# Ternary weights prepared by compares on GpSimd and means on ScalarE, and a timetable three times as fine, in a state-space and feed-forward kernel

## The chip, the core and the metric

The kernel runs on one core of a Trainium2 chip. The core has five engines, each with an instruction queue of its own that it works through in order: TensorE (PE, matrix products, with the loading of its weights shown apart as PEld), VectorE (DVE), ScalarE (ACT), GpSimd (POOL) and SyncE (SP, which here only issues DMAs). They meet through semaphores alone: an instruction that needs a result waits at the head of its queue, and all that stands behind it waits too. The metric is the device time of one execution in microseconds, the median of the runs.

## The reference

The input is x[2, 4096, 256] in float32. Two layers with residuals are applied:

```
x = x + layernorm(ssm(layernorm(x)))
x = x + layernorm(ffn(layernorm(x)))
```

The state-space layer projects to 2 x 512 channels (a path x and a gate z) and takes B, C (16 states each), dt and lam from silu(x). For each of 512 channels and 16 states it runs, over 4096 tokens, `h = dA*h + u`, and y is the sum over states of `h*C`. Then y is gated with silu(z) and projected back to 256. The feed-forward layer is 256 to 1024 to 256 with gelu and a layernorm between, and its weights are ternary:

```python
def ternary_quant(w):
    scale = 1.0 / jnp.clip(jnp.mean(jnp.abs(w)), 1e-05)
    wq = jnp.clip(jnp.round(w * scale), -1.0, 1.0) / scale
    return w + jax.lax.stop_gradient(wq - w)
```

So each weight becomes -1, 0 or 1 times the mean magnitude of its matrix.

## The kernel before, in words

**Blocks and units.** The 8192 tokens are cut into 16 blocks of 512 (`NB`), 8 to a batch. In a block the scan covers 512 channels x 16 states, that is 64 *units* of 128 rows by 512 tokens (`NU` = 64): 4 channel quarters j, times 4 groups q of states, times 4 units c. A group is four units. For each unit ACT computes the decays `da` = exp(A dt) into PSUM (`decay`, L924, by `special`, L217; `da` has four buffers). For each pair of units POOL multiplies B and v into a group's tile `g` (`inputs`, L929, instruction L934; three buffers). DVE then runs one hardware scan per unit (`unit_scan`, L940): for the first `SPLIT[q]` units of a group (2, 1, 2, 1) it writes into `da` (L947), for the others into `g` (L950). The product with C is DVE's for the former (`product_v`, L964, and a copy of the last column, L965) and POOL's, in place in `g`, for the latter (`product_g`, L960), after ACT has copied their last column to `hl` (`last`, L954). PE adds up the states (`sum_states`, L976, into `y`), which frees the `g` tile, and DVE gates (`gate`, L986). `start_y` (L970) puts the skip term into `y` first.

**The rest of a block** is put between the units: for the block after the next layernorm, projections, softplus, rotation and so on (`plan_ahead`: `a_stats`, `project`, `keep`, `silu_x`, ..., `load_c`), and for the block before the output projection and the feed-forward layer (`plan_behind`: `out_project`, `out_square`, `residual`, `h_stats`, `ffn_1`, `ffn_keep`, `gelu`, `ffn_2`, `ffn_sums`, `ffn_out`, ..., `finish`). dt, v, B and C go through HBM and come back spread over the rows (`load_ch`: dtr and vr; `load_bc`: b and c); SP issues those DMAs in program order.

**What sets the order.** The queues' order is written out by hand. The main loop (L1312) goes from unit to unit. At each it asks for the decays up to 3 units and the inputs of up to 3 units ahead (`AHEAD_DA`, `AHEAD_U`), issues the scan, then what lags (`behind`, L1265, with one lag in units for each kind in `LAG`), and then every piece of the plans whose unit has come (`AT`, `AT_FIRST` for block 0, `W_AT` for the weights; `Plan.run`, L1119).

**The weights.** In block 0 a third plan (`plan_weights`, L1242) prepares the constant weights between the units. `centre_out` (L355) takes from each row of `wo` its mean. `ternary` (L369) loads a matrix into half of a wide tile, takes the mean magnitude (ACT with an accumulator, then a PE product with ones), and on DVE rounds by adding and subtracting a large constant, clips, scales, and forms w + (wq - w). `weights_1` and `weights_2` then fold in the layernorms' gains (`gains`) and offsets (`offsets`, PE), and for the second matrix subtract the mean over the hidden axis (`hidden_mean`, `centre`) and over the outputs (`output_mean`, `finish`, instruction L481). All of that elementwise work is on DVE.

Of the kernel before, what the change touches and what calls it, by code (L numbers as in the profile page):

```python
# [8 lines left out]
F32 = mybir.dt.float32  # L9
# [5 lines left out]
P = 128  # L15
# [23 lines left out]
AHEAD_DA, AHEAD_U = 3, 3  # L39
# [3 lines left out]
LAG = {"product_v": 2, "last": 4, "product_g": 5, "gate": 9, "start": 7, "sum": 8}  # L43

W_AT = (11, 13, 20, 23, 24, 24, 27, 28, 28, 30, 33, 33, 38, 41, 46, 51, 51, 51, 52, 52, 55, 58, 59, 62, 63)
LOAD_FIRST = 8
AT = {
    "a_stats": (2, 2),
    "a_power": (2,),
    "a_offset": (3,),  # L50
    "a_apply": (3, 4),
    "a_turn": (4, 5),
    "a_evict": (5, 5),
    "project": (5, 7, 11, 11, 19, 21, 21, 21),
    "keep": (7, 9, 11, 13, 20, 21, 22, 24),
    "silu_x": (13,),
    "bc_project": (17, 17),
    "bc_take": (19,),
    "dt_project": (25,),
    "bc_square": (22,),  # L60
    "bc_power": (24,),
    "dt_row": (30,),
    "dt_spread": (33,),
    "softplus": (33,),
    "bc_scale": (33,),
    "dt_turn": (35, 35, 35, 37),
    "dt_keep": (35, 35, 36, 37),
    "dt_sum": (43,),
    "angles": (43,),
    "diag_lam": (29,),  # L70
    "diag_rem": (29,),
    "silu_z": (49,),
    "sines": (49,),
    "rotate_a": (52,),
    "rotate_b": (52,),
    "bc_turn": (52,),
    "bc_store": (54,),
    "dot_sum": (53,),
    "dot_shift": (53,),
    "dot_take": (60,),  # L80
    "weigh": (37, 37, 46, 46),
    "weigh_x": (39, 39, 47, 50),
    "over": (49,),
    "over_x": (52,),
    "spread": (60,),
    "carry": (61,),
    "diag_dot": (64,),
    "skip": (64, 66, 67, 67),
    "skip_x": (65, 66, 67, 67),
    "load_dt": (41,),  # L90
    "load_v": (40,),
    "load_b": (59, 59, 58, 61),
    "load_c": (55, 59, 59, 64),
    "x_load": (5,),
    "out_project": (12, 12),
    "out_square": (16, 16),
    "out_power": (16, 16),
    "residual": (18, 18),
    "h_stats": (18, 18),
    "h_power": (18,),  # L100
    "h_offset": (20,),
    "h_apply": (20, 20),
    "h_turn": (21, 25),
    "h_evict": (24, 25),
    "ffn_1": (25, 29, 31, 31, 34, 34, 41, 42),
    "ffn_keep": (27, 29, 31, 32, 34, 34, 42, 42),
    "gelu": (40, 45),
    "ffn_2": (47, 50, 52, 62),
    "ffn_sums": (48, 52, 57, 64),
    "ffn_out": (48, 52, 58, 65),  # L110
    "ffn_square": (60, 58, 63, 66),
    "ffn_power": (60, 66),
    "ffn_scale": (62, 66),
    "finish": (64, 66),
# [9 lines left out]
    "project": (-59, -58, -57, -56, 0, 0, 0, 0),  # L124
    "keep": (-58, -57, -56, -55, 0, 0, 0, 0),
# [16 lines left out]
    "silu_z": (2,),  # L142
# [8 lines left out]
    "weigh": (-41, 0, 2, 0),  # L151
    "weigh_x": (-35, 0, 3, 4),
    "diag_dot": (0,),
    "skip": (0, 4, 4, 4),
    "skip_x": (2, 5, 5, 5),
    "load_dt": (-34,),
    "load_v": (-32,),
    "load_b": (-31, -20, 0, 0),
    "load_c": (-30, -20, 0, 0),
# [4 lines left out]
def mamba_ffn_kernel(  # L164
# [190 lines left out]
    def centre_out():  # L355
        wom = small.tile([P, NJ], F32, tag="rows", name="wom")
        nc.vector.tensor_reduce(wom, wo, AX.X, ALU.add)
        nc.vector.tensor_scalar_mul(wom, wom, 1.0 / DM)
        for j in range(NJ):
            nc.vector.tensor_scalar_sub(wo[:, j, :], wo[:, j, :], wom[:, j : j + 1])  # L360
# [8 lines left out]
    def ternary(src, wide, nk, width):  # L369
# [27 lines left out]
        def round_():  # L397
            nc.vector.tensor_scalar(q, w, t["scale"], ROUND, ALU.mult, ALU.add)
            nc.vector.tensor_scalar(q, q, ROUND, -1.0, ALU.subtract, ALU.max)

        def clip():
            nc.vector.tensor_scalar(q, q, 1.0, t["inv"], ALU.min, ALU.mult)

        def apart():
            nc.vector.tensor_sub(q, q, w)

        def together():
            nc.vector.tensor_add(w, w, q)

        return w.rearrange("p (k n) -> p k n", k=nk), [  # L410
            load, magnitude, total, scales, round_, clip, apart, together,
        ]

    def weights_1(wide):
        w, steps = ternary(w1T, wide, 2, HID)
        t = {}

        def offsets():
            t["pb"] = mm_tile([P, NH], "pb1")
            for f in range(NH):  # L420
                for kk in range(2):
                    nc.tensor.matmul(
                        t["pb"][:, f : f + 1],
                        lhsT=w[:, kk, f * P : (f + 1) * P],
                        rhs=lb1[:, kk : kk + 1],
                        start=(kk == 0),
                        stop=(kk == 1),
                    )

        def gains():  # L430
            nc.vector.tensor_add(b1c, t["pb"], b1c)
            for kk in range(2):
                nc.vector.tensor_scalar_mul(w1q[:, kk, :], w[:, kk, :], g1[:, kk : kk + 1])

        return steps + [offsets, gains]

    def weights_2(wide):
        w, steps = ternary(w2T, wide, NH, DM)
        t = {}

        def offsets():
            t["pb"] = mm_tile([P, DM], "pb2")
            for f in range(NH):
                nc.tensor.matmul(
                    t["pb"],
                    lhsT=lb2[:, f : f + 1].to_broadcast([P, P]),
                    rhs=w[:, f, :],
# [4 lines left out]
        def gains():  # L452
            nc.vector.tensor_add(b2bc, t["pb"], b2bc)
            for f in range(NH):
                nc.vector.tensor_scalar_mul(w[:, f, :], w[:, f, :], g2[:, f : f + 1])
# [10 lines left out]
        def centre():  # L466
            m = p1.tile([P, DM], F32, tag="junk", name="m2")
            nc.vector.tensor_scalar_mul(m, t["pm"], 1.0 / HID)
            nc.vector.tensor_sub(w, w, m[:, None, :].to_broadcast([P, NH, DM]))

        def output_mean():
            wm = small.tile([P, NH + 1], F32, tag="wm", name="wm", bufs=1)
            nc.vector.tensor_reduce(wm[:, 0:NH], w, AX.X, ALU.add)
            nc.vector.tensor_reduce(wm[:, NH : NH + 1], b2bc, AX.X, ALU.add)
            nc.vector.tensor_scalar_mul(wm, wm, 1.0 / DM)
            t["wm"] = wm

        def finish():
            wm = t["wm"]
            for f in range(NH):  # L480
                nc.vector.tensor_scalar_sub(w2q[:, f, 0:DM], w[:, f, :], wm[:, f : f + 1])  # L481
            nc.vector.tensor_scalar_sub(b2bc, b2bc, wm[:, NH : NH + 1])

            nc.vector.memset(w2q[:, :, DM : DM + 1], 1.0)

        return steps + [offsets, gains, hidden_mean, centre, output_mean, finish]
# [625 lines left out]
    class Plan:  # L1112
# [6 lines left out]
        def run(self, unit):  # L1119
            while self.pieces and self.pieces[0][0] <= unit - self.start:  # L1120
                self.pieces.pop(0)[2]()
# [5 lines left out]
    def plan_ahead(s, prev):  # L1127
# [3 lines left out]
        else:  # L1131
            plan = Plan(AT, prev.k * NU)
# [64 lines left out]
    def plan_behind(s):  # L1197

        plan = Plan(AT, (s.k + 1) * NU)
# [65 lines left out]
    def behind(m):  # L1265
# [121 lines left out]
```

## Time and profile before

| | |
|---|---|
| median of 3 runs | 2062.05 us (2061.23 to 2062.91) |
| profiled execution | 2063.1 us, its span 2061.4 us |
| first scan of block 0 | 64.5 us |
| first scan of block 1 | 224.3 us |
| last scan | 1983.0 us |
| busy DVE, POOL, PE, ACT | 1799.0, 1791.1, 1741.9, 1622.9 us |
| DVE's scans, L950 and L947 | 706.1 and 423.0 us |
| POOL's inputs L934 and products L960 | 1017.4 and 631.7 us |
| ACT's decays, L217 da | 690.3 us |

The span is that of the instructions on the chip; the execution's time has 1.7 us around it. A row of the profile is a group of like instructions: line, engine, operation, tiles written and read, shapes, count, then busy time and mean duration in ns, then the idle time of that engine just before them and who ended it. A wait is written "A <- B": A stood until B was done.

### The profile page before, as it was taken

To read this page: it belongs to the slowest core of one execution; us is meant where nothing else is said; L and a number is where in the kernel's file an instruction comes from. 1 tells how busy PE (TensorE), PEld (TensorE's weight loads), DVE (VectorE), ACT (ScalarE), POOL (GpSimd) and SP (SyncE) were. 2 spreads that over 40 slices of the span, in tenths; PEclk is the share of its full clock that TensorE was granted. 3 is DMA by queue.
4 is the path that set the end of the run, shared out by engine and by line. 5 is a ranking of instruction groups with operands and counts; after the bars stand their busy time and mean duration, and the time that the engine had idled before them with its cause. 6 is when DMAs were issued, how large, how long until landed. Compare 5 with 4: busy or idle time off the path is not lost.

```text
span 2061.4 us, 28008 instructions
## 1 busy us (share of the span) xinstructions
PE 1741.9 (85%) x8638; PEld 1040.5 (50%) x8638; DVE 1799.0 (87%) x2806; ACT 1622.9 (79%) x3301; POOL 1791.1 (87%) x1163
## 2 busy tenths in 40 slices
PE   6765788998898898988889899988888898888677
PEld 3423446464554546455454646455454645555255
DVE  1789989899899989999898989989898999989950
ACT  5655587888979798888979788897979888796743
POOL 3578799998999999999999999999999999999950
PEclk7867799999999999999999999999999999998899
DMA  4832536444564545445463644446454544556200
GB/s 80 203 82 74 129 78 153 112 106 111 126 153 100 137 105 135 110 114 134 123 147 86 151 112 114 110 121 150 107 131 109 132 109 110 136 123 142 44 21 10
DMA packets 155687, 233.37 MB, mean 113 GB/s; under 512 B 30129, under 2 KB 55793, under 8 KB 155537
## 3 DMA queue, kind: packets, MB, share of 16 engines
q1 hardware_dynamic: 153408, 230.80, 46.6%
q0 software_dynamic: 544, 0.71, 0.2%
q8 instruction: 68, 1.11, 0.2%
q14 instruction: 83, 0.67, 0.1%
q10 hardware_dynamic: 1584, 0.07, 0.1%
HBM read 188.51 MB, written 42.99 MB: 112 GB/s over the span
## 4 chain that ended last, share of the span: by engine, by line
DVE 37%; ACT 31%; PE 11%; issue 9%; DMA 6%; POOL 5%; SPq 1%; DVEq 0%; POOLq 0%; ACTq 0%
DVE g L950 15%; ACT da L217 10%; DVE da L947 8%; ACT L217 4%; DVE g L964 4%; ACT L213 3%; DMA vr<-v_d 3%; ACT h L217 3%; POOL g L960 2%; PE ph L1022 2%; PE pf L1044 2%; DMA xpre<-in_L_attn_x_dram 2%; POOL g L934 2%; ACT dt L217 2%; ACT zs L217 1%
## 5 line engine op out<-in xcount | busy, mean ns | idle before, releaser
L934 POOL TENSOR_TENSOR g<-b,vr 128x1024 f32<-128x1024 f32 x512 | 1017.4, 2001 | 13.3 <-DMA c<-bc_d 13.3
L217 ACT ACTIVATE da<-dtr,aneg 128x512 f32<-128x512 f32 x1024 | 690.3, 685 | 191.2 <-DVE g L950 183.5
L960 POOL TENSOR_TENSOR g<-c,g 128x1024 f32<-128x1024 f32 (+1 forms) x256 | 631.7, 2468 | 108.6 <-ACT hl L954 105.3
L950 DVE TENSOR_TENSOR_SCAN g<-da,ini,g 128x512 f32<-128x512 f32 x560 | 706.1, 1267 | 3.5 <-ACT da L217 3.5
L947 DVE TENSOR_TENSOR_SCAN da<-da,ini,g 128x512 f32<-128x512 f32 x336 | 423.0, 1279 | 72.4 <-POOL g L934 43.9
L1044 PE MATMUL pf<-w2q,h 128*128 128x257 f32 x1024 | 315.7, 390 | 39.9 <-DVE o L1082 26.0
L976 PE MATMUL y<-g,fold 128*32 128x512 f32 x2048 | 312.0, 639 | 42.9 <-ACT y L970 23.8
L562 PE MATMUL pz<-oT_a,wi 128*128 128x512 f32 x512 | 275.1, 677 | 30.9 <-ACT zs L576 28.7
L1022 PE MATMUL ph<-oT_h,w1q 128*128 128x512 f32 x512 | 259.6, 645 | 37.3 <-ACT dt L217 33.7
L964 DVE TENSOR_TENSOR g<-da,c 128x512 f32<-128x512 f32 x384 | 255.6, 666 | 0.0
L1053 PEld LDWEIGHTS pf<-h 128*128 128x128 f32 x1024 | 195.3, 191 | 27.5
L1053 PE MATMUL pf<-h 128*128 128x128 f32 x1024 | 197.4, 275 | 0.0
L562 PEld LDWEIGHTS pz<-oT_a,wi 128*128 128x128 f32 x512 | 101.9, 214 | 182.6 <-issue 95.2
L1022 PEld LDWEIGHTS ph<-oT_h,w1q 128*128 128x128 f32 x512 | 93.9, 197 | 187.2 <-issue 90.0
L1044 PEld LDWEIGHTS pf<-w2q,h 128*128 128x128 f32 x1024 | 155.7, 192 | 57.2 <-DVE o L1082 36.0
L976 PEld LDWEIGHTS y<-g,fold 128*32 128x32 f32 x2048 | 46.0, 110 | 160.6 <-POOL g L960 41.5
L815 PE MATMUL pw<-ddot,dtT 128*128 128x128 f32 (+1 forms) x512 | 85.7, 317 | 43.2 <-DVE dx L878 27.4
L994 PE MATMUL po<-wo,zs 128*128 128x256 f32 x512 | 116.8, 387 | 0.0
L994 PEld LDWEIGHTS po<-wo,zs 128*128 128x128 f32 x512 | 97.4, 193 | 28.0 <-ACT da L217 5.0
L217 ACT ACT_TABLE_LOAD x80 | 102.6, 1283 | 1.4
L815 PEld LDWEIGHTS pw<-ddot,dtT 128*128 128x128 f32 x512 | 73.2, 212 | 60.4 <-DVE dx L878 28.8
L213 ACT ACT_TABLE_LOAD x80 | 102.6, 1283 | 1.2
(206 smaller groups left out, 2375.0 us busy)
## 6 DMA issues: line engine op xcount, KB each, us to landing
dtr<-dt_d SPq DMA_DIRECT2D x256, 256.0 KB, 5.5
vr<-v_d SPq DMA_DIRECT2D x256, 256.0 KB, 7.3
dt_d<-dt SPq DMA_DIRECT2D x64, 256.0 KB, 3.9
v_d<-v SPq DMA_DIRECT2D x64, 256.0 KB, 2.1
b<-bc_d SPq DMA_DIRECT2D x256, 64.0 KB, 2.1
c<-bc_d SPq DMA_DIRECT2D x256, 64.0 KB, 2.2
xpre<-in_L_attn_x_dram SPq DMA_DIRECT2D x16, 512.0 KB, 4.5
xpost<-in_L_attn_x_dram SPq DMA_DIRECT2D x16, 512.0 KB, 3.9
```

Of the source, the lines that this page charges most:

```text
L217: nc.scalar.activation(dst, src, f, **kw)
L562: nc.tensor.matmul(s.pz[e], lhsT=wi[:, kk, e * P : (e + 1) * P], rhs=s.na.oT[:, kk, :], start=(kk == 0), stop=(kk == 1),)
L934: nc.gpsimd.tensor_mul(s.g[j, q][:, hs, :], s.bcq[0, q][:, None, :].to_broadcast([P, 2, T]), s.ch[j, "vr"][:, hs, :],)
L947: nc.vector.tensor_tensor_scan(da, da, g, ini, ALU.mult, ALU.add)
L950: nc.vector.tensor_tensor_scan(g, da, g, ini, ALU.mult, ALU.add)
L960: nc.gpsimd.tensor_mul(g, s.bcq[1, q][:, None, :].to_broadcast([P, NG - n, T]), g)
L964: nc.vector.tensor_mul(s.g[j, q][:, c, :], da, s.bcq[1, q])
L976: nc.tensor.matmul(s.ys[j][c * G : (c + 1) * G, :], lhsT=fold, rhs=g[:, c, :], start=False, stop=(q == NQ - 1), skip_group_check=True,)
L994: nc.tensor.matmul(s.p2[h][:, i, :], lhsT=s.zs[j][:, c * P : (c + 1) * P], rhs=wo[:, j, :], start=(j == 0), stop=(j == NJ - 1),)
L1022: nc.tensor.matmul(s.ph[f], lhsT=w1q[:, kk, f * P : (f + 1) * P], rhs=s.nh.oT[:, kk, :], start=(kk == 0), stop=(kk == 1),)
L1044: nc.tensor.matmul(po[:, 0 : DM + 1], lhsT=gT, rhs=w2q[:, f, :], start=(f == 0), stop=(f == NH - 1), skip_group_check=True,)
L1053: nc.tensor.matmul(po[:, DM + 1 :], lhsT=gT, rhs=gT, start=False, stop=False, skip_group_check=True,)
```

## The change

**The weights.** With s the scale, round(s w) clipped to -1..1 is the compare s w > 0.5 less the compare s w < -0.5. Both compares (128x2048) and their difference (two halves) are now made by GpSimd; the factor 1/s is not multiplied into the matrix but into the gains and the offsets (`factors`, a few columns). The form w + (wq - w) goes. The gains are applied by ScalarE, which sums each row in the same instruction (`accum_out`), so that the separate reductions over the outputs go too; the mean of a row after centring is that sum less the sum of the hidden mean. ScalarE also takes the means of `wo` and subtracts means (as a bias). VectorE keeps the scale, two additions of biases and one subtraction of the hidden mean, now in one instruction that reads PSUM.

**The timetable.** A unit now has three places: before the decays and inputs ahead are issued, between them and the scan, and after the scan; a block has 192. All tables are written in places. The lags of `last`, `product_g` and `sum` differ from group to group, those of `gate` and `start` from quarter to quarter. Decays and inputs are asked for 2 units ahead instead of 3.

```diff
-AHEAD_DA, AHEAD_U = 3, 3
+AHEAD_DA, AHEAD_U = 2, 2
-LAG = {"product_v": 2, "last": 4, "product_g": 5, "gate": 9, "start": 7, "sum": 8}
-LOAD_FIRST = 8
+LAG = {
+    "product_v": (6,),
+    "last": (24, 19, 23, 11, 15, 14, 19, 20, 16, 12, 17, 15, 12, 14, 15, 11),
+    "product_g": (31, 20, 29, 21, 24, 21, 23, 22, 23, 16, 22, 20, 19, 16, 17, 20),
+    "gate": (33, 32, 31, 33),
+    "start": (28, 24, 25, 26),
+    "sum": (36, 29, 29, 26, 29, 22, 26, 27, 33, 23, 27, 24, 30, 25, 27, 30),
+}
+W_AT = (17, 24, 60, 69, 70, 79, 90, 90, 110, 117, 122, 122, 129, 129, 129, 130, 133, 133, 136, 136, 137, 137, 138, 143, 147, 153, 169, 175, 185)
+LOAD_FIRST = 6
 AT = {
...
-    "silu_x": (13,),
+    "silu_x": (42,),
-    "softplus": (33,),
+    "softplus": (89,),
-    "out_square": (16, 16),
-    "out_power": (16, 16),
-    "residual": (18, 18),
+    "out_square": (46, 48),
+    "out_power": (48, 48),
+    "residual": (50, 51),
-    "ffn_keep": (27, 29, 31, 32, 34, 34, 42, 42),
-    "gelu": (40, 45),
+    "ffn_keep": (84, 92, 111, 114, 117, 118, 126, 127),
+    "gelu": (116, 133),
-    "ffn_sums": (48, 52, 57, 64),
-    "ffn_out": (48, 52, 58, 65),
+    "ffn_sums": (143, 156, 172, 190),
+    "ffn_out": (143, 158, 173, 191),
...
     def centre_out():
...
+            nc.scalar.activation(
+                junk, wo[:, j, :], AF.Copy, scale=-1.0 / DM, accum_out=wom[:, j : j + 1]
+            )
+        for j in range(NJ):
+            nc.scalar.activation(wo[:, j, :], wo[:, j, :], AF.Identity, bias=wom[:, j : j + 1])
...
+        def above():
+            nc.gpsimd.tensor_scalar(q, w, t["scale"], 0.5, ALU.mult, ALU.is_gt)
+
+        def below():
+            nc.gpsimd.tensor_scalar(w, w, t["scale"], -0.5, ALU.mult, ALU.is_lt)
+
+        def signs(half):
+            n = NH * DM // 2
+            hs = slice(half * n, half * n + n)
+            nc.gpsimd.tensor_sub(q[:, hs], q[:, hs], w[:, hs])
+
+        def factors():
+            for name, col in cols.items():
+                t[name] = small.tile([P, nk], F32, tag=f"wc{nk}{name}", name=name, bufs=1)
+                nc.gpsimd.tensor_scalar(t[name], col, t["inv"], None, ALU.mult)
...
+            for f in range(4 * h, 4 * h + 4):
+                nc.scalar.activation(
+                    w[:, f, :],
+                    q[:, f, :],
+                    AF.Copy,
+                    scale=t["g"][:, f : f + 1],
+                    accum_out=t["row"][:, f : f + 1],
+                )
...
+            nc.vector.scalar_tensor_tensor(
+                w,
+                t["pm"][:, None, :].to_broadcast([P, NH, DM]),
+                -1.0 / HID,
+                w,
+                ALU.mult,
+                ALU.add,
+            )
...
+    def at_place(place):
+        behind(place)
+        for plan in plans:
+            plan.run(place)
...
+        at_place(3 * base)
+        if cur is not None:
             ahead(base + AHEAD_DA, "da", 1, decay)
             ahead(base + AHEAD_U, "u", 2, inputs)
+        at_place(3 * base + 1)
+        if cur is not None:
             unit_scan(cur, j, q, c)
-        behind(base)
-        for plan in plans:
-            plan.run(base)
+        at_place(3 * base + 2)
```

`behind` now looks a place up in a table `due`, made once from `LAG`. The other entries of `AT` and `AT_FIRST` are all rewritten in the same way: most move by a few units, softplus and what hangs on it three to six units earlier, the last two `weigh` some sixteen later; the z projections and the skips of block 0 move from its first unit to within its first six.

## The prediction, made before the result

> **What bounds the kernel now.** I read the page first. Four engines are busy for 79 to 87% of the span, so no total decides, and each stage has to be read by itself.
>
> ```profile
> span 2061.4 us, 28008 instructions
> PE 1741.9 (85%) x8638; PEld 1040.5 (50%) x8638; DVE 1799.0 (87%) x2806; ACT 1622.9 (79%) x3301; POOL 1791.1 (87%) x1163
> ```
>
> Next the busy time by stretch, cut at the first scan of block 0 (64.5 us), of block 1 (224.2), of one later block (578.3 to 696.9), and of the last block (columns: stretch, its length, then busy time and count of PE, PEld, DVE, ACT, POOL, then the granted clock).
>
> ```profile
> 64.50:224.20 159.70, 101.27 (x439) 59.96 (x437) 148.12 (x199) 85.64 (x159) 125.86 (x67) 0.71 0.42 106
> 578.30:696.90 118.60, 105.67 (x542) 63.22 (x538) 109.76 (x173) 100.77 (x207) 110.25 (x72) 0.96 0.50 121
> 1875.00:1983.00 108.00, 80.37 (x376) 44.67 (x376) 101.74 (x145) 71.69 (x149) 103.17 (x54) 0.86 0.33 73
> ```
>
> By the starts of every 64th scan, blocks 1 to 14 take 1650.8 us (117.9 each), the last 107.9, and from its last scan to the end there are 78 us. A middle block has 109.8 us of DVE and 110.3 of POOL work: both are all but full, and 8 us of the block are waits. Block 0 has 148 us on DVE and 42 us more length than the others: it carries the weights.
>
> Whose waits they are, over the six blocks 342 to 1050 us (columns: total, times, longest); first DVE's own, then POOL's largest.
>
> ```profile
> DVE da L947 <- POOL g L934: 19.6, 12, 1.7
> DVE da L947 <- ACT da L217: 11.2, 12, 1.5
> DVE o L1082 <- ACT rsf L217: 9.6, 12, 0.8
> DVE zs L986 <- PE y L976: 1.7, 3, 1.0
> ```
> ```profile
> POOL g L960 <- ACT hl L954: 33.1, 32, 1.9
> ```
>
> Per block: 3.3 us for POOL's inputs, 1.9 for ACT's decays, 1.6 for ACT's root, 0.6 others. POOL loses 5.5 us at its products, waiting for ACT's copy of the last column, which stands behind decays that wait for DVE: a ring.
>
> Last, the weights in block 0 (lines of 64.5 to 224.2 us), and what they do to POOL meanwhile:
>
> ```profile
> L481 DVE TENSOR_SCALAR w2q<-wide,wm 128x256 f32<-128x256 f32 x8 | 6.6, 891 | 0.0
> L408 DVE TENSOR_TENSOR wide<-wide 128x2048 f32<-128x2048 f32 x2 | 6.4, 3178 | 0.0
> L360 DVE TENSOR_SCALAR wo<-wo,wom 128x256 f32<-128x256 f32 x4 | 6.3, 1639 | 0.0
> ```
> ```profile
> 130.20 4.04 POOL L960 TENSOR_TENSOR g<-c,g 128x1024 f32<-128x1024 f32 x1
> 134.21 3.22 POOL L802 TENSOR_TENSOR mix<-mix,ident 128x512 f32<-128x512 f32 x1
> 517.94 1.18 POOL L802 TENSOR_TENSOR mix<-mix,ident 128x512 f32<-128x512 f32 x1
> ```
>
> The first two ran while DVE did the 128x2048 operations of w1 (129.4 to 136.3 us); the third is the same instruction in a later block. The 256-wide L360 and L481 took 1.64 and 0.89 us where L455, of that size, took 0.35: the two engines hold each other up.
>
> **Part 1, the weights (block 0).** Removed from DVE by the rows of that stretch: L481 6.6, L408 6.4, L360 6.3, L405 5.2, L398 3.2, L402 2.7, L399 2.5, L473 2.3, L455 2.2, L433 2.0, L358 1.4, L357 1.2 and four small ones (L468, L474, L482, L475) 1.3: 43.3 us. The subtraction of the hidden mean stays (3.5 us, now straight from PSUM), as do the scales and two bias adds. DVE in block 0: 148.1 - 43.3 = 104.8 us.
>
> Added to ACT: 4 sums of 256 (0.40 + 0.19 for the accumulator, row L1091) and 4 corrections (0.50, L1102) of wo; 2 products of 1024 (1.1, from 0.67 for 512 in L1033); 8 products with sums (0.69), 2 means (0.57), 9 corrections (0.50): 18 us. ACT: 85.6 + 18 = 104, beside the rest.
>
> Added to POOL: four compares of 128x2048, four subtractions of 128x1024 (2.00, row L934) and seven small ones (1.4): 9.4 us and the compares. No row has such a compare. Below: POOL's COPY took 0.29 us for 128 and 0.61 for 512 columns, which gives 1.9 for 2048. Above: its TENSOR_SCALAR took 0.22 for 32 and 0.55 for 128, which gives 7.2; but that 0.55 lay beside DVE's three adds of `fold`, one of which took 0.33 instead of 0.19. A two-input row gives 4.0 (twice 2.00). I take 3.0, between the copy and the two-input row, and keep 1.9 and 7.2. Weights on POOL: 9.4 + 12.0 = 21.4. What POOL gets back is its slowing by DVE's weights: 1.0 + 2.0 + 2.0 on g, 2.0 on mix, 0.8 on bc, 5.0 + 1.9 on cs, t and bdotc (2.36 us for one that takes 0.32): 14.8. POOL in block 0: 125.9 - 14.8 + 21.4 = 132.5 us, the longest of the four. It also waits: for the scale of w2, behind its load (landing 5.7 to 13.6 us), ACT's magnitude (1.9) and PE; for ACT's row sums; at its products. Behind the first compare of w2 stand POOL's inputs of units 46 to 49, and DVE's scans wait for those. I take 7 us, a middle block's (33.1 us at L960 and 11 in small ones over six blocks), bounds 3 and 12. Block 0: 139.5 instead of 159.7, **20 us less**; bounds 29 less (1.9 a compare, 3 of waits) and 2 more (7.2 and 12).
>
> A rule speaks against this part. The Trainium skill, "GPSIMD Engine Reference", section Engine selection, sends elementwise work to VectorE and calls GpSimd about twice as slow with two inputs, near line rate with one. The trace agrees on two inputs (2.00 us for 1024 on POOL, 2.3 at best for 2048 on DVE, L405). By the page alone the compares would be about 1.8 us each, an estimate, and block 0 some 5 us shorter than mine; the engine that is full decides here. "SBUF — State Buffer", section "Who interferes with whom", says that VectorE in a two-port mode or with two SBUF inputs locks GpSimd out; the 3.22 us against 1.18 shows it.
>
> **Part 2, the timetable (15 blocks).** Not one operation of a middle block changes, only the order on the queues, so its floor stays at 110.3 us. I laid both kernels' queues for one block side by side and added up the rows' durations.
>
> *DVE waiting for POOL (3.3 us).* If both queues ran without gaps, from the first input and scan on, POOL's inputs before would come up to 2.4 us late (unit 36), while the fourth group's product stands 0.1 us too early for its scan: no shift between the engines serves both, 2.5 us are lost, 3.3 are measured. In the new order the worst are 2.3 (unit 56) and a product with 1.2 us in hand: 1.1. The last column's copy now stands one to ten places before its product instead of one unit. I take 1.6 off; bounds 0 and 3.3.
>
> *DVE waiting for decays (1.9).* 1.4 of it is unit 16: silu of x (table, 1.91, copy, table: 4.7 us of ACT) stood one unit before it. It now stands before da 15, and out_square behind da 16; counting ACT's rows from the scan that frees da 14's buffer, da 15 comes at 6.1 us and its scan can start at 6.3. 1.4 off, with no slack (bounds 0 and 1.9).
>
> *Root (1.6).* Two of four ffn_out stood right behind ffn_sums; now one does: 0.8 off (bounds 0 and 1.6).
>
> *New.* Products move back, from 5 units behind to 16 to 31 places (three to a unit), so a g buffer comes free later. Between a group's product and the inputs that reuse its buffer POOL had at least 5.9 us of other work, and now 2.0 (groups 6 and 7), 2.9 and 3.0 (0 and 2). In it PE must do four y matmuls (the last six of the trace take 1.9 us). I add 0.8; bounds 0 and 4.0 (2.0 at two groups).
>
> Sum: -1.6 - 1.4 - 0.8 + 0.8 = -3.0 a block, 42 for fourteen, 1.5 for the last: **43.5 us less**. SP's queue: its loads of b, c, dtr and vr keep their order within a few units and land before use in both lists; v of quarters 2 and 3 is stored some 15 units later, yet behind the loads that units 16 on need and 14 units ahead of its own; nothing taken. Start: z projections and skips move to either side of the first scan, which waits 11.9 us for inputs anyway, and dtr and vr of the next quarter are asked for two units sooner: nothing, bounds 3 either way. Tail (78 us): gelu 0 goes ahead of ffn_keep 4; PE then stands 2 us for a buffer and gelu 1 ends as before: nothing, bounds 3.
>
> **The sum.** The profiled execution took 2063.1 us, 1.7 outside its span; 2063.1 - 20.2 - 43.5 = 1999.4. The median of the runs is 1.05 below the profiled one: 1998.
>
> **Rivals.**
> *The timetable only moves the waits.* Both engines are 93% full, so a wait removed in one place may return at the next. Against it: the margins above. 2062 - 20 = 2042. Chance 0.14.
> *The compares are dear.* At 7.2 us or more POOL is the bound of block 0 at 161 us. For it: the one row of that operation. 2062 - 43 = 2019. Chance 0.13.
> *PE late with the sums (slower).* With a g buffer held longer, POOL waits wherever PE comes late to the y matmuls. For it: PE waited up to 3.3 us for ACT's softplus (ph, 19.5 us in six blocks), and group 6's sum now stands behind the dt turns that need it. Against: that group's product starts 5.2 us after its last scan, when the softplus should be past. At 2.5 us for four groups POOL loses 10 a block, 5 more than it saves: 2062 + 70 - 20 = 2112. It decides from 5.2 us a block on (the 3.8 saved, and 20/14). Chance 0.10.
> *It does nothing*: the weights' chain eats what DVE gives up and the order is neutral: 2062. Chance 0.03.
>
> **How the numbers follow.** Both gains: 0.60, at 1998. The cheapest ends (6.7 a block, 29 in block 0) give 1936, the dearest of the likely case about 2045. 1945 to 2045 leaves out some 0.05 below and 0.13 above. A measurement here can tell 0.2% (4 us). Faster 0.87, same 0.03, slower 0.10.
>
> **What would show it.** After: first scan of block 0 to that of block 1 near 140 us, with DVE near 105 and POOL near 132 busy; compares of about 3 us; mix at 1.2 in block 0; middle blocks near 115 us with their busy time unchanged; "DVE da <- POOL g" near 1.7 a block, unit 16's wait gone, "POOL g <- ACT hl" far below 5.5. I am wrong if POOL shows a large wait for PE y, if the compares exceed 5 us, or if POOL stands long for the scale of w2.

## The result, and the profile after

The changed kernel takes 2061.14 us (median of 12 runs, 2057.33 to 2064.41), the kernel before, beside it, 2061.23 (12 runs, 2059.81 to 2062.91). The ratio is 0.9999, its 95% interval 0.9990 to 1.0008: no difference that can be measured, where 1998 was forecast. Ratios, here and below, are of fast runs: one of the five runs of fused_keep took 3213.1 us and is in none of them.

The page of the changed kernel, its span and its busy times:

```profile
span 2059.2 us, 28149 instructions
PE 1742.7 (85%) x8638; PEld 1036.3 (50%) x8638; DVE 1761.0 (86%) x2766; ACT 1627.1 (79%) x3344; POOL 1815.7 (88%) x1178
```

DVE has lost 38.0 us, POOL has gained 24.6, and the span is 2.2 us shorter (one execution of each kernel). By stretch, cut at the first scans of block 0 (64.3 us), block 1 (228.9), block 4 (580.9) and block 5 (700.0), and at those of the last block (columns: stretch, length, busy time and count of PE, PEld, DVE, ACT, POOL, granted clock):

```profile
64.30:228.90 164.60, 95.32 (x372) 54.26 (x371) 104.07 (x156) 95.51 (x192) 143.89 (x80) 0.66 0.40 101
580.90:700.00 119.10, 106.18 (x541) 63.43 (x540) 110.10 (x174) 100.11 (x207) 110.31 (x72) 0.96 0.50 123
1873.30:1981.00 107.70, 80.81 (x393) 44.10 (x391) 101.83 (x145) 71.21 (x144) 103.25 (x54) 0.90 0.32 77
```

Block 0 is 4.9 us **longer** than before (164.6 against 159.7), although DVE has 44 us less work in it. Blocks 1 to 14 take 228.9 to 1873.3 us, 117.46 each instead of 117.9: 6.4 us less in all. The first scan stands at 64.3 (64.5 before), from the last scan to the end there are 78.2 us (78.4). So both parts failed to pay, each for a reason of its own: block 0 was to lose 20 us, the middle blocks 3.0 us each. Of the forecast gain, 25 us are missing in block 0 and 36 in blocks 1 to 14.

Waits of block 0 in the changed kernel, DVE's largest (columns: total, times, longest), and then POOL's groups of the weights there (busy time, mean ns, idle before):

```profile
DVE da L997 <- POOL g L984: 23.8, 4, 9.2
DVE b2bc L476 <- PE pb L466: 15.8, 1, 15.8
DVE g L1000 <- ACT da L225: 8.8, 4, 3.6
DVE g L1000 <- POOL g L984: 6.6, 2, 6.2
```
```profile
L410 POOL TENSOR_SCALAR wide<-wide,scale 128x2048 f32<-128x2048 f32 x2 | 14.4, 7179 | 2.1 <-ACT hl L1004 2.1
L413 POOL TENSOR_SCALAR wide<-wide,scale 128x2048 f32<-128x2048 f32 x2 | 14.3, 7162 | 0.0
L852 POOL TENSOR_TENSOR mix<-mix,ident 128x512 f32<-128x512 f32 x1 | 1.2, 1178 | 0.0
```

DVE now stands where it used to work. (Of the 23.8 us, 6.0 lie ahead of the first scan, outside the stretch; the kernel before waits 11.9 there.) Each compare (L410, L413) takes 7.2 us and holds up POOL's inputs, for which the scans wait: 5.7 us at unit 28, 9.2 at unit 32, 6.2 at unit 46; the compares of the second matrix also hold up its offsets on PE, and DVE's addition of those (L476) stands in its queue ahead of the scans. `mix`, which took 3.22 us beside DVE's weights before, takes 1.18.

Waits over the six blocks 345.6 to 1052.5 us, DVE's and POOL's:

```profile
DVE g L1000 <- ACT da L225: 14.3, 17, 1.9
DVE da L997 <- POOL g L984: 7.9, 6, 2.1
DVE da L997 <- ACT da L225: 5.0, 9, 0.6
DVE o L1132 <- ACT rsf L225: 4.8, 6, 0.8
DVE g L1000 <- ACT hl L1004: 4.2, 6, 0.7
DVE g L1000 <- POOL g L984: 2.6, 7, 1.6
```
```profile
POOL g L1010 <- ACT hl L1004: 20.3, 26, 1.6
POOL g L984 <- PE y L1026: 3.8, 7, 1.2
```

Per block: waits of DVE for POOL's inputs 1.75 us (3.3 before), for the root 0.8 (1.6), but for ScalarE's decays 3.2 (2.0: the 1.9 of L947 and 0.2 at L950), and a new one of 0.9 behind ScalarE's copy of the last column (0.7 in the row shown, the rest at L997).

### The profile page after: what moved, and what is told of

Its sections match the earlier page's. It is cut to its first block, busy times and chain, and to the rows that moved or that the text cites. A ratio compares the mean times of both kernels' runs of the same rounds, so it can differ in the third digit from the quotient of the medians.

```text
span 2059.2 us, 28149 instructions
## 1 busy us (share of the span) xinstructions
PE 1742.7 (85%) x8638; PEld 1036.3 (50%) x8638; DVE 1761.0 (86%) x2766; ACT 1627.1 (79%) x3344; POOL 1815.7 (88%) x1178
## 4 chain that ended last, share of the span: by engine, by line
ACT 38%; DVE 17%; POOL 12%; DMA 11%; PE 11%; issue 8%; SPq 3%; DVEq 0%; ACTq 0%; POOLq 0%
ACT da L225 12%; POOL g L984 6%; DVE g L1000 6%; DMA vr<-v_d 6%; ACT L225 5%; DVE da L997 4%; ACT L221 3%; DMA xpre<-in_L_attn_x_dram 3%; ACT h L1083 3%; POOL g L1010 2%; ACT dt L225 2%; PE pdtT L733 2%; PE y L1026 2%; ACT h L225 2%; DVE g L1014 2%
## 5 line engine op out<-in xcount | busy, mean ns | idle before, releaser
L997 DVE TENSOR_TENSOR_SCAN da<-da,ini,g 128x512 f32<-128x512 f32 x336 | 422.0, 1274 | 33.2 <-POOL g L984 17.8
L1026 PE MATMUL y<-g,fold 128*32 128x512 f32 x2048 | 338.7, 662 | 42.3 <-POOL g L1010 32.2
L612 PE MATMUL pz<-oT_a,wi 128*128 128x512 f32 x512 | 251.0, 627 | 10.4 <-ACT zs L626 4.9
L612 PEld LDWEIGHTS pz<-oT_a,wi 128*128 128x128 f32 x512 | 92.9, 195 | 158.6 <-issue 87.3
L1000 DVE TENSOR_TENSOR_SCAN g<-da,g 128x512 f32<-128x512 f32 x80 | 96.5, 1211 | 19.7 <-ACT da L225 11.7
L865 PE MATMUL ps<-mix,dtT 128*128 128x129 f32 (+1 forms) x512 | 81.3, 306 | 34.2 <-DVE remdot L833 27.0
```

The costliest lines, as they stand in the source:

```text
L612: nc.tensor.matmul(s.pz[e], lhsT=wi[:, kk, e * P : (e + 1) * P], rhs=s.na.oT[:, kk, :], start=(kk == 0), stop=(kk == 1),)
L997: nc.vector.tensor_tensor_scan(da, da, g, ini, ALU.mult, ALU.add)
L1000: nc.vector.tensor_tensor_scan(g, da, g, ini, ALU.mult, ALU.add)
L1026: nc.tensor.matmul(s.ys[j][c * G : (c + 1) * G, :], lhsT=fold, rhs=g[:, c, :], start=False, stop=(q == NQ - 1), skip_group_check=True,)
```

## The experiments

All times are in us; "blocks" is the mean length of blocks 1 to 14 in the profiled run. The kernel before took 2061.5 to 2063.2 in the four groups of runs, and each ratio is against the runs of its own group. The profiled run of compares_dve, 2046.99, was the longest of its five.

| run | time | ratio, 95% interval | block 0 | blocks |
|---|---|---|---|---|
| before | 2061.23 | | 159.8 | 117.9 |
| after | 2061.14 | 0.9999 (0.9990 to 1.0008) | 164.7 | 117.5 |
| timetable_alone | 2076.25 | 1.0072 (1.0058 to 1.0086) | 172.6 | 117.6 |
| weights_alone | 2072.87 | 1.0056 (1.0044 to 1.0069) | 170.7 | 117.9 |
| compares_dve | 2041.84 | 0.9908 (0.9892 to 0.9923) | 143.1 | 117.8 |
| cheap_pool | 2037.12 | 0.9881 (0.9867 to 0.9894) | 139.3 | 117.5 |
| fused_dve | 2034.12 | 0.9866 (0.9852 to 0.9879) | 133.6 | 117.6 |
| first_z | 2068.53 | 1.0034 (1.0022 to 1.0046) | 166.2 | 117.6 |
| da3 | 2206.76 | 1.0706 (1.0692 to 1.0721) | 169.3 | 127.4 |
| keep_later | 2045.21 | 0.9916 (0.9902 to 0.9929) | 161.3 | 116.3 |
| best | 2057.83 | 0.9982 (0.9973 to 0.9990) | 137.9 | 119.1 |
| fused_keep | 2015.87 | 0.9768 (0.9754 to 0.9781) | 133.8 | 116.2 |
| fk_angles | 2050.04 | 0.9935 (0.9920 to 0.9951) | 134.0 | 118.8 |
| fk_out | 2021.58 | 0.9797 (0.9784 to 0.9810) | 132.0 | 116.7 |

**The price of a compare (battery, battery2).** Added behind the end of the changed kernel:

```diff
...
+    nc.gpsimd.tensor_copy(bq, bw)                                          # L1409
...
+    nc.gpsimd.tensor_scalar(bq, bw, 0.5, None, ALU.is_gt)                  # L1411
+    nc.gpsimd.tensor_scalar(bq, bw, 2.0, 0.5, ALU.mult, ALU.add)           # L1412
+    nc.gpsimd.tensor_scalar(bq, bw, dsk[:, 0:1], None, ALU.mult)           # L1413
+    nc.gpsimd.tensor_scalar(bq, bw, dsk[:, 0:1], 0.5, ALU.mult, ALU.is_gt) # L1414
+    nc.gpsimd.tensor_sub(bq, bw, bw)                                       # L1415
...
```

> The changed kernel with nine GpSimd instructions of 128x2048 float32 added behind its end, with nothing beside them on the other engines: a fill, a copy, multiplication by a constant, a compare with a constant, multiplication and addition by constants, multiplication by a value per row, multiplication by such a value and compare (the form of the change), a subtraction of two inputs, a product with a broadcast column. Theory A1: the price goes with the second operation; the one-operation forms take about 2 to 4 us and both two-operation forms about 7.2. Theory A2: it goes with the value per row: the two forms that read one take about 7.2, the others 2 to 4. Theory A3: any TENSOR_SCALAR of this size takes about 7.2 and only copy and fill are cheap (1.9 by the slope of the small copies). Theory A4: the 7.17 us in block 0 came from sharing memory with VectorE: then the form of the change takes about 4 here.

Groups of POOL at the end of that run:

```profile
L1414 POOL TENSOR_SCALAR bat<-bat,dsk 128x2048 f32<-128x2048 f32 x1 | 7.2, 7164 | 0.1
L1413 POOL TENSOR_SCALAR bat<-bat,dsk 128x2048 f32<-128x2048 f32 x1 | 5.4, 5446 | 0.1
L1411 POOL TENSOR_SCALAR bat<-bat 128x2048 f32<-128x2048 f32 x1 | 5.4, 5371 | 0.1
L1415 POOL TENSOR_TENSOR bat<-bat 128x2048 f32<-128x2048 f32 x1 | 3.6, 3601 | 0.1
L1412 POOL TENSOR_SCALAR bat<-bat 128x2048 f32<-128x2048 f32 x1 | 1.9, 1900 | 0.1
L1409 POOL COPY bat<-bat 128x2048 f32<-128x2048 f32 x1 | 1.9, 1891 | 0.1
```

A4 falls: with nothing beside it the change's form takes the same 7.16 us as in block 0. A1 to A3 fall too, each in a row: one operation (L1411, L1413) is dearer than the two of L1412, which cost no more than a copy. A second battery tried what makes the fast form.

> More forms of GpSimd's TENSOR_SCALAR behind the end of the changed kernel, on 128x2048 float32: product with a value per row and sum with a constant; product with a constant and compare; product with a constant and maximum; sum and product with constants in the other order; and the form of the change on 1024, 512 and 128 columns. Theory F (one fast form, product and then sum, 1.9 us; all else pays per operation): the first and the fourth take 1.9 to 3, or only the first does, those with compare or maximum about 7.2; the form of the change scales with its columns, 3.6, 1.8 and 0.5 us. Rival V (the value per row is part of the price): the first takes 3.5 or more although it is product and sum, and the compare with constants is below 7.

Here L1409 is a product with a value per row and a sum, L1410 a product and a compare with constants, L1415 the change's form on 128 columns:

```profile
L1410 POOL TENSOR_SCALAR bat<-bat 128x2048 f32<-128x2048 f32 x1 | 7.1, 7104 | 0.1
L1409 POOL TENSOR_SCALAR bat<-bat,dsk 128x2048 f32<-128x2048 f32 x1 | 2.0, 1972 | 0.1
L1415 POOL TENSOR_SCALAR bat<-bat,dsk 128x128 f32<-128x128 f32 x1 | 0.7, 714 | 0.1
```

Theory F: product and sum together, in either order and with or without a value per row, took 1.90 to 1.97 us; with a compare or a maximum 7.08 to 7.16. The form of the change took 3.71, 2.00 and 0.71 us on 1024, 512 and 128 columns: the first and second as F said, the third above its 0.5, since some 0.3 us do not scale.

**The price alone (cheap_pool).**

```diff
-            nc.gpsimd.tensor_scalar(q, w, t["scale"], 0.5, ALU.mult, ALU.is_gt)
+            nc.gpsimd.tensor_scalar(q, w, 0.5, 0.5, ALU.mult, ALU.add)
-            nc.gpsimd.tensor_scalar(w, w, t["scale"], -0.5, ALU.mult, ALU.is_lt)
+            nc.gpsimd.tensor_scalar(w, w, -0.5, 0.5, ALU.mult, ALU.add)
```

> The changed kernel with its four compares on GpSimd replaced by a product and a sum with constants, which took 1.90 us for 128x2048 in the battery where the compare took 7.16. The weights then are not the ternary ones and neither is the output; all other instructions and their order are those of the changed kernel. Theory A (price alone): GpSimd sheds 4 x 5.26 = 21 us in block 0, which lies on the path, and block 0 falls from 164.7 to 142 to 146 us, the time to 2038 to 2044, as with the compares on VectorE. Rival C (it is the handing over between the engines, which the compares on VectorE took away as well): block 0 falls by less than 10 us, time 2051 or more.

Theory A, and a little more than it said. The same queues with the four instructions at 1.90 us; block 0 by stretch, columns as above:

```profile
64.50:203.80 139.30, 92.80 (x375) 51.07 (x375) 103.94 (x157) 95.91 (x193) 122.71 (x80) 0.72 0.46 120
```

POOL's work falls by the 21.2 us of the price, block 0 by 25.4: the price and some of what queued behind it (DVE's wait for PE's offsets, L476, fell from 15.8 to 9.0). Block 0 is then within 0.2 us of the predicted 139.5. (These four no longer wait for the scale either; in the changed kernel POOL waited 2.1 us ahead of one of them, which the profile puts down to `hl`.)

**The compares on VectorE (compares_dve).** The two lines with `nc.vector` for `nc.gpsimd`.

> The changed kernel with its four compares on VectorE, nothing else moved. Theory A (the compares' price on GpSimd carries the loss): GpSimd loses 28.7 us of work in block 0, VectorE gains 5 to 6 (by its two-operation row of that size before the change, 1.6 us, or 1.25), and block 0 falls by the 20 to 25 us between the price taken and the price paid, to 140 to 145 us: time 2036 to 2042. Rival C: the chain of the second matrix (load, scale, compares, factors, offsets on TensorE, and the bias addition on VectorE for which its scans wait 18 us) sets block 0, and the compares are only 14 us of it, half of them covered: block 0 falls by 5 to 10 us, time 2051 to 2056.

Block 0 fell by 21.5 us, theory A again. Three of VectorE's four compares, with GpSimd idle, took 1.26 to 1.29 us; the first of L410, beside GpSimd's products and inputs, took 2.35, and an input there 2.98 instead of 2.00. Its wait for PE's offsets halved but did not go, and of its 10.7 us for POOL's inputs 6.2 lie ahead of the first scan:

```profile
DVE da L997 <- POOL g L984: 10.7, 3, 6.2
DVE b2bc L476 <- PE pb L466: 7.9, 1, 7.9
```

**One part alone (weights_alone, timetable_alone).** The new weights with the old timetable, their pieces at units 11, 13, 20, 23, 24, 24, 27, 28, 28, 28, 30, 33, 33 and 33, 38, 41, 46, 51, 51, 51, 52, 52, 52, 55, 55, 58, 59, 62, 63; and the new timetable with the old weights, at their old units.

> The old timetable with the new weights, each piece at the unit where the old piece stood that it replaces. Theory A (the compares' price): four compares of 7.17 us put GpSimd's busy time in block 0 near 149 us, it waits some 15 to 20 us besides, and block 0 takes 164 to 170 us; blocks 1 to 14 stay at 117.9. Time 2066 to 2072. Rival B (the new order spoils block 0, the weights are neutral or help): block 0 is 150 to 160 us, time 2051 to 2061.

> The changed timetable with the old weights on VectorE (their pieces at the same units as before the change). Theory A: block 0 lost its gain to the price of the compares on GpSimd (7.17 us each where 3.0 was taken), and the timetable is worth what blocks 1 to 15 show, 6.6 us. Then block 0 is about 160 us from first scan to first scan, as before the change, and the time about 2054 us, 7 below both kernels. Rival B: the new order is what spoils block 0 (its z projections, skips and loads have new places there too). Then block 0 stays near 165 us without any compare on GpSimd, and the time is 2060 to 2062.

The weights alone cost 11 us, a little more than theory A said (block 0 170.7 for its 164 to 170). The timetable alone cost 15 us, and there theory A failed and rival B fell short: its middle blocks gained only 0.3 us each, and block 0 took 172.6 us without a compare on GpSimd. Block 0 by stretch, and DVE's waits in it:

```profile
64.70:237.30 172.60, 95.91 (x370) 53.67 (x369) 152.73 (x197) 83.28 (x152) 123.69 (x66) 0.68 0.38 95
```
```profile
DVE g L958 <- ACT da L225: 8.4, 4, 3.6
DVE da L955 <- ACT da L225: 0.9, 1, 0.9
```

DVE is busy for 152.7 of 172.6 us, 4.6 more than before, because the two engines hold each other up more. The gains of the second matrix (first the kernel before, then this run) took 0.34 us each with GpSimd idle and up to 2.17 beside its inputs:

```profile
L455 DVE TENSOR_SCALAR wide<-wide,g 128x256 f32<-128x256 f32 x8 | 2.2, 346 | 0.0
L463 DVE TENSOR_SCALAR wide<-wide,g 128x256 f32<-128x256 f32 x8 | 7.1, 956 | 0.0
```

The rest is DVE's waits: 9.3 us for decays, where the kernel before shows 3.1 in its block 0 (one wait, at unit 36), and 2.4 at unit 20, which the profile puts down to nothing. The largest (unit 7 3.6, unit 20 2.4, unit 34 3.0) stand at the same units in the changed kernel (3.6, 2.4, 3.4). The trace of the changed kernel has unit 7's behind ScalarE's copy of a z projection, which waited 2.2 us for PE (5.8 in the timetable alone), and unit 20's scan begins as the first decay behind the silu of z ends: a burst of 4.8 us with two table loads, which the new timetable moves from unit 2 to unit 19. So the two halves were not additive: +14.6 and +11.2 alone, nothing together. A likely reason is that with the old weights DVE fills block 0 and pays for these waits and for the slowing, while with the new ones it has 44 us less to do. But both halves also kept the old units of the weights' pieces; no run has the change's own (`W_AT`) with one half alone, so their share is not shown.

**The z work of block 0 put back (first_z).**

```diff
-    "project": (-59, -58, -57, -56, 16, 2, 2, 0),
-    "keep": (-58, -57, -56, -55, 18, 3, 5, 0),
-    "silu_z": (57,),
+    "project": (-59, -58, -57, -56, 0, 0, 0, 0),
+    "keep": (-58, -57, -56, -55, 0, 0, 0, 0),
+    "silu_z": (8,),
```

> The changed kernel with block 0's z projections, copies and silu of z back at the places of the kernel before; nothing else. In the changed kernel VectorE waits 3.6 us at unit 7 and 2.4 and 1.6 at units 20 and 21 for decays that stand behind those copies and that silu on ScalarE. Theory D (those waits are on the path of block 0): block 0 falls from 164.7 to 157 to 160 us, time 2053 to 2057. Rival P (GpSimd with its compares sets block 0 in this kernel, and VectorE only waits for it longer at units 28 to 46): block 0 stays at 163 to 166, time 2058 to 2064.

Block 0 went from 164.7 to 166.2 us, the upper edge of rival P, and the time 4.5 us above its range: the waits at units 20 and 21 (3.9 us) shrank to 1.6, but 2.6 came at unit 4 and 1.3 at unit 21 for `lam`, unit 12's grew from 2.9 to 4.2, and unit 7's stayed (3.1 for 3.6). So that wait does not hang on the z copy alone: ScalarE's silu of z, now at 73 us, and its sums and corrections of `wo` stand ahead of the decay there. Why the blocks after it were 0.2 us longer each was not looked into.

**The sign in two instructions on VectorE (fused_dve).**

```diff
-            nc.gpsimd.tensor_scalar(q, w, t["scale"], 0.5, ALU.mult, ALU.is_gt)
+            nc.vector.tensor_scalar(q, w, t["scale"], 0.5, ALU.mult, ALU.is_gt)
-            nc.gpsimd.tensor_scalar(w, w, t["scale"], -0.5, ALU.mult, ALU.is_lt)
+            nc.vector.scalar_tensor_tensor(q, w, t["edge"], q, ALU.is_lt, ALU.subtract)
...
-            nc.gpsimd.tensor_sub(q[:, hs], q[:, hs], w[:, hs])
```

> A candidate: VectorE makes the first compare and then, in one instruction, the second compare (against -0.5/scale) less the first, which is the sign with its sign turned; the factors are multiplied by -1 as well, and GpSimd's subtractions go. GpSimd loses four compares (28.7 us) and four subtractions (9.4) in block 0, VectorE gains two compares (1.2 to 1.6 each) and two fused ones (2.3 by its 128x2048 row that reads PSUM). Theory A (GpSimd's queue sets block 0 up to the second matrix): block 0 falls from the 143 us of the compares on VectorE to 133 to 138, time 2031 to 2036. Rival C (the chain of the second matrix and VectorE's waits for decays set the rest): 140 to 144, time 2038 to 2043.

Theory A: block 0 133.6 us, DVE 113.9 and POOL 110.3 busy. The fused instruction took 3.35 us, not the 2.3 of the row that it was judged by; both times it began 0.8 us behind the start of a GpSimd input (2.0 us), and no run has it with GpSimd idle:

```profile
L415 DVE SCALAR_TENSOR_TENSOR wide<-wide,edge 128x2048 f32<-128x2048 f32 x2 | 6.7, 3349 | 0.0
```

**One more decay in hand (da3).**

```diff
-AHEAD_DA, AHEAD_U = 2, 2
+AHEAD_DA, AHEAD_U = 3, 2
```

> The changed kernel with decays asked for 3 units ahead, as before the change, instead of 2; its inputs stay at 2. Theory S1 (the waits of VectorE for decays at units 15, 31 to 34, 46 and 52, 4.0 us a block, come from bursts of ScalarE for silu, softplus and gelu that one more decay in hand would cover): VectorE loses 1.0 us less per unit affected, 2 to 3 a block, time 2016 to 2031. Rival S2 (GpSimd and VectorE are a full ring in which a wait taken away comes back elsewhere): middle blocks stay at 117 to 118, time 2057 to 2065. Rival S3 (the fourth decay buffer comes free too late, and ScalarE stands at the head of its queue with other work behind it): 1 to 2 us a block more, time 2075 to 2090.

S3, at five to ten times its size: 9.9 us a block. ACT's waits for DVE over six blocks, first of da3, then of the changed kernel:

```profile
ACT da L225 <- DVE g L1000: 52.3, 41, 3.1
ACT da L225 <- DVE hl L1015: 39.8, 30, 3.4
```
```profile
ACT da L225 <- DVE g L1000: 10.5, 23, 1.0
ACT da L225 <- DVE hl L1015: 10.2, 6, 1.7
```

A decay needs the buffer of the one four units back; where the scan has written into that, it comes free with DVE's product and copy of the last column (L1015), two units behind that scan. Asked for three units ahead, it stands at the head of ACT's queue until DVE has just done that, and gelu, roots and last columns stand behind it; POOL's products waited 146.7 us for ACT's last columns in the whole run, 55.0 in the changed kernel. So the 2 of the change goes with its lags: the kernel before asked for 3.

**A new wait taken away (keep_later).** In the changed kernel ACT's fourth copy of the turned dt stands for PE in every middle block:

```profile
646.31 0.60 ACT L741 ACTIVATE dtT<-pdtT 128x512 f32<-128x512 f32 x1 [1.68 <-PE pdtT L733]
```
```diff
-    "dt_keep": (91, 96, 97, 99),
+    "dt_keep": (95, 98, 102, 106),
```

> The changed kernel with ScalarE's four copies of the turned dt put 4, 2, 5 and 7 places later (95, 98, 102, 106 instead of 91, 96, 97, 99), so that TensorE has time to turn: in every middle block ScalarE stands 1.5 us at unit 34 for the last turn, and VectorE 1.3 us for the decays behind it. Theory S1: that wait of VectorE goes and nothing takes its place, 1.3 us a block: time 2038 to 2046. Rival S2 (full ring): the waits come back at other units, the block stays within 0.4 us, time 2056 to 2066.

Theory S1: 16 us faster than the changed kernel, 1.1 a block, and 3.4 in block 0, where the 3.4 us wait of DVE at unit 34 fell to 0.9 as well; the last block became 2.2 longer. DVE's waits over six blocks:

```profile
DVE cum L755 <- PE pa L717: 8.8, 6, 2.0
DVE g L1000 <- ACT da L225: 6.2, 12, 0.8
DVE da L997 <- POOL g L984: 5.5, 6, 0.9
DVE o L1132 <- ACT rsf L225: 4.8, 6, 0.8
```

The waits for decays fell from 19.3 to 6.6 us. In part another took their place: 1.5 us a block for the sum of dt, at unit 37.

**Two more waits taken away (best, fk_angles, fk_out, fused_keep).** On the fused sign and the later copies, the angles and the first ffn_out were moved:

```diff
-    "angles": (110,),
+    "angles": (122,),
-    "ffn_out": (143, 158, 173, 191),
+    "ffn_out": (147, 158, 173, 191),
```

> The fused sign on VectorE together with: ScalarE's copies of the turned dt put later as in the run before; the angles 12 places later (122 instead of 110), because in that run VectorE stood 1.6 us a block for their sum; the first ffn_out 4 places behind its sums instead of beside them (VectorE stood 0.8 us a block for ScalarE's root); and in block 0 the z projections, their copies and silu of z back at the places of the kernel before (0 and 8 instead of 2 to 18 and 57). Theory S1 (these waits are on the path): middle blocks fall from 116.2 to 114 to 115 us; block 0 falls from 133.6 by the 6.5 us of VectorE's waits at units 7, 20 and 21, to 126 to 130: time 1985 to 2005. Rival S2 (a floor near 116, as VectorE's 110 and GpSimd's 110 us of work need some 6 us of waits for each other): middle blocks stay at 116 to 116.5, time 2008 to 2018.

Both theories missed: the middle blocks took 119.1 us, 2.8 more than in fused_keep, and block 0 137.9 (132.0 to 134.0 in the runs without first_z's places). The four runs tell the moves apart: `best` has both and first_z's places, fk_angles and fk_out one each, fused_keep none.

> The fused sign on VectorE and ScalarE's copies of the turned dt put later (95, 98, 102, 106), and nothing of the other moves. If the two gains are independent, since one lies in block 0 and the other in the blocks after it: block 0 134 to 137 us (133.6 with the fused sign; keep_later's own block 0 was 3.4 shorter than the changed kernel's, which may be the same wait), middle blocks 116.2, time 2016 to 2021. If not (the state in which block 0 ends decides which waits the blocks after it show): middle blocks 117 or more, time 2027 or more.

> The same with the angles at 122 instead of 110, which alone took away VectorE's 1.6 us wait at unit 37. Theory S4 (the removed wait comes back in the next places, because GpSimd and ScalarE were due at that time and not sooner, and the seven small operations of the angles now stand between scans that are already late): units 38 to 41 show 3 us of waits for g and da, middle blocks 117.5 to 118.5, time 2036 to 2050. Rival S5 (the later ffn_out is what lost the 3 us): middle blocks 114.6 to 116, time 1995 to 2016.

> The same with only the first ffn_out 4 places later, which took away VectorE's 0.8 us wait at unit 48. Theory S4: the PSUM tile that ffn_out frees comes free later, TensorE is late with the next of its sums, VectorE waits for that at unit 52 (1.0 us) instead of for the root, and the block is 116.2 to 117.5, time 2016 to 2036. Rival S5: it is this move that lost the 3 us: middle blocks 118.5 to 119.5, time 2050 to 2065.

fused_keep came as the sum of its two gains, 2015.87 us: block 0 as in fused_dve, the blocks as in keep_later. The later ffn_out cost 0.4 a block, as S4 said: the 0.8 us for the root became 0.5 for `v` and 1.0 for PE's sums (units 49 and 52). It was the angles that lost 2.5, a little more than S4 said (118.8 for its 117.5 to 118.5). DVE around unit 37, first of fused_keep, then of fk_angles, and ACT of fk_angles:

```profile
616.65 0.16 DVE L750 COPY cum<-pa 128x4 f32<-128x4 f32 x1 [1.33 <-PE pa L712]
...
618.34 1.27 DVE L995 TENSOR_TENSOR_SCAN g<-da,ini,g 128x512 f32<-128x512 f32 x1
```
```profile
624.80 1.28 DVE L995 TENSOR_TENSOR_SCAN g<-da,ini,g 128x512 f32<-128x512 f32 x1 [0.80 <-POOL g L979]
...
629.86 1.29 DVE L992 TENSOR_TENSOR_SCAN da<-da,ini,g 128x512 f32<-128x512 f32 x1 [2.01 <-ACT da L225]
631.06 0.15 DVE L750 COPY cum<-pa 128x4 f32<-128x4 f32 x1
```
```profile
623.98 1.28 ACT L225 ACT_TABLE_LOAD   x1
625.27 1.91 ACT L225 ACTIVATE h<-h 128x2048 f32<-128x2048 f32 x1
627.09 0.67 ACT L1078 ACTIVATE h<-ph,b1c 128x512 f32<-128x512 f32 x1
627.78 1.28 ACT L221 ACT_TABLE_LOAD   x1
629.07 0.69 ACT L225 ACTIVATE da<-dtr,aneg 128x512 f32<-128x512 f32 x1
```

From 623.98 to 629.07 ACT is at gelu, and no decay is made; DVE lives on those in hand, up to unit 39. In fused_keep the same burst runs from 616.93 to 622.03, but there the wait at unit 37 and the angles behind it have kept DVE from its scans for 3.0 us (1.33 of waiting, 1.69 from 616.65 to 618.34), and unit 40 starts at 623.14 without a wait. With the angles behind the next scans, these come sooner, find POOL's input 0.8 us late and then the decay 2.0 us late, and the angles are still to be done. Over blocks 1 to 14 the 1.45 us a block at unit 37 became 1.34 at unit 38, 1.54 at unit 40, and 1.0 more at units 3 and 28.

## Why the prediction was wrong, by its steps

**The price of the compares, the term that was mis-sized.** 3.0 us was taken, "between the copy and the two-input row", with 1.9 and 7.2 as bounds; it measured 7.17. The upper bound came from rows of the same instruction, and it was set aside because 0.55 us for 128 columns "lay beside DVE's three adds of `fold`": alone the change's form takes 0.71 there. That the bound met the price was luck all the same. Its rows hold other arithmetic, a product and a sum on 32 columns (L727) and a single product on 128 (L261), and on 2048 columns these two forms take 1.90 and 5.39. With 7.17 the sum gains 4 x 4.17 = 16.7 us and comes to 156.2; the prediction's own sign, compares above 5 us, came true.

**POOL's waits in block 0.** 7 was taken from a middle block, bounds 3 and 12; it was 20.7 (164.6 less 143.9). Of that, 7.2 us ahead of the layernorm of block 1 and 3.7 for a load stand before 82 us, at the start of block 0; POOL of the kernel before shows a wait of 7.4 at that first place too, and the step did not read it. POOL's work was 5.3 less than the sum gives with 7.17 (143.9 for 149.2), most of it because one input (2.0) and one product (2.9) fewer fall into the stretch. So 156.2 + 13.7 - 5.3 = 164.6. That block 0 still met 139.5 us once the compares cost 1.9 is luck, two errors that cancel: 122.7 of work and 16.6 of waits, for 132.5 and 7.

**What held in part 1.** DVE's 43.3 us left (104.1 busy; 104.8 foretold), and the two engines no longer hold each other up (mix 1.18). ACT's 18 us show as 9.9 more in its block 0; where the rest went was not looked into. Taking that work from DVE does pay: block 0 is 139.3, 143.1 and 133.6 us in cheap_pool, compares_dve and fused_dve, for 159.8. The reason was right and the place of the compares was not.

**Part 2, step by step.** "DVE waiting for POOL", 1.6 off: 3.3 became 1.75. "Root", 0.8 off: 1.6 became 0.8. "New", 0.8 for PE's sums: 3.8 in six blocks, 0.6. These three held. **"DVE waiting for decays", 1.4 off "with no slack", failed**: 1.9 (2.0 with the row at L950 that the step left out) became 3.2, and 0.9 came behind `hl`, for which the sum had no term. These 2.1 us took back most of the 2.3 gained at POOL's inputs and the root, and the block lost 0.46 us instead of 3.0. The step followed one burst (silu of x, unit 16) and not the other three on the same queue, softplus with the turns of dt, gelu, and silu of z; the change moved all of them. The wait at unit 16 became one of 0.85 at unit 15, and units 31 to 34 got 2.2. keep_later shows that a few places' shift takes most of this last away, for a gain of 1.1 a block, since 1.5 came at unit 37. POOL's waits for `hl`, foretold "far below 5.5", were 3.4 a block.

**Start.** "Nothing, bounds 3": true of the first scan, not of what follows. The timetable alone made block 0 12.8 us longer, 4.6 of it in DVE's own work. The z work put back did not shorten block 0 (first_z), so which of the moved entries cost it stays open.

**The rivals.** Two of them came true at once. "The compares are dear" named 161 us for block 0 (164.7 came), "the timetable only moves the waits" no gain (0.46 us a block came). Each was priced by itself, 2019 and 2042; both together are no gain at all, about 2062, and that case stood only as "it does nothing", with another cause. "PE late with the sums" did not happen.

The rule of the Trainium skill that part 1 was weighed against, in "GPSIMD Engine Reference", section Engine selection, sends elementwise work to VectorE. The runs agree with that advice: the same compare took 1.26 to 1.29 us there with GpSimd idle, and 2.35 beside it. Its remark that GpSimd runs about at line rate with one input agrees with the copy (1.89 us) and with product and sum (1.90), and not with the compares (7.16) or a single product (5.39). Its factor of about two against VectorE for two inputs came out smaller: 3.60 us for a subtraction of 128x2048, where VectorE's took 2.29 at best (L405 of the kernel before).

## What to carry to other kernels

When bounds lie far apart, measure the form itself, operations and size, with a few lines behind the end of the kernel: the same instruction on the same shape cost 1.9 to 7.2 us here, by its arithmetic alone. Reckon independent rivals together as well as one by one. In a full ring of engines a wait is worth its length only if what stands behind it is late for no other reason: look at what the other engines do during the wait, because a stop of one may be the cover of another's burst.

## What the hardware showed that was not expected

GpSimd's TENSOR_SCALAR on 128x2048 float32 has a fast form: product and sum, 1.90 us with constants and 1.97 with a value per row. A single product or a single compare took 5.4, a product with a compare or a maximum 7.1 to 7.2: two operations can cost a third of one. VectorE's compare (L410 of compares_dve) took 1.29 us with GpSimd idle and 2.35 beside its products, and a GpSimd input at that time 2.98 instead of 2.00. VectorE's L502 of the changed kernel, with one input from PSUM, ran beside a GpSimd input at no cost to that (2.29 and 2.00). The best version found, fused_keep, stands at 0.9768 of the kernel before (0.9754 to 0.9781), with the compares on VectorE and ScalarE's copies of dt a few places later.
